# A graph network of 32 batch entries: eight groups of four become two, seven times four, and two

## The chip, the cores and the metric

The kernel runs on one core of one Trainium2 chip. The metric is the device time of one execution in microseconds (us). Before the change the median of 3 runs is 3128.19 us (3117.14 to 3134.04). A difference under 0.5% can't be told from no change.

A core has engines with instruction queues of their own, each worked off in order: PE (TensorE, matrix products; PEld is its weight load), DVE (VectorE), ACT (ScalarE), POOL (GpSimd) and SP (which only issues transfers). Transfers are issued from SP, ACT and POOL. POOL alone issues the indirect ones, which gather or scatter rows by a list of indices.

## What is computed

The input x has 32 batch entries of 512 nodes by 256 features; one adjacency matrix adj of 512 x 512 serves all of them, and about 1.6% of it is not zero besides its diagonal. Four layers follow one another:

```python
def gnn(h, A, W1, b1, W2, b2, Wa, ba, Wm, bm, beta1, beta2, beta3):   # layers 0 and 3
    pre_u, pre_v = h @ W1[:256], h @ W1[256:]
    hidden = relu(pre_u[:, :, None] + pre_v[:, None] + b1)             # per entry 512 x 512 x 256
    S = sigmoid(hidden @ W2 + b2)                                      # per entry 512 x 512
    a = einsum('buv,bud->bvd', S * A, h)
    m = einsum('uv,bud->bvd', A, h) * h
    return beta1 * h + beta2 * (a @ Wa + ba) + beta3 * (m @ Wm + bm)

x = gnn(x, adj, ...)                                                   # layer 0
x = x + relu((adj @ x) @ W.T + b)                                      # layer 1
f = x @ W1.T; g = f @ W2 + b2                                          # layer 2
x = softmax(leaky_relu(g[:, None] + g[None]) + adj) @ f + bias2 + x
x = gnn(x, adj, ...)                                                   # layer 3
```

S is needed only where adj is not zero, since it is multiplied by adj. The kernel computes it there alone, edge by edge.

## The kernel before

The 32 entries go in eight groups of four (`NB` = 4). A group passes through these stages; each is a Python generator, and each of its `yield`s ends a piece of instructions:

- `first` loads four entries of x, turns them on PE and calls `pre`, which computes pre_u and pre_v and writes them to a table in DRAM (`table`, one row per node, the four entries side by side: 4 KB a row). 16 table writes a group, from SP.
- `edges` (layer 0: `edges0`) computes S on the edges. The edges are held as 36 *items* of 128 edges (`ITEMS`): 32 from lists of each node's neighbours, and 4 from *panels*, which hold what overflows. The 36 don't depend on the size of the group: an edge list serves all entries, and a larger group only makes the rows longer. For each item POOL issues a gather (`fetch`, L607), DVE adds the two ends (L686), applies relu and W2 (L694 for all four entries at once, with the sums on ACT, L672; or L702 entry by entry with the sum on DVE), a sigmoid follows for some items together, and POOL issues a scatter (`put`, L601) of 128 values per entry into `cells`. These are two dense arrays in DRAM, one for each half of the rows of S*adj. The scatters of one half follow one another, each waiting for the landing of the one before it. The panels need a gather more each, for the other end of their edges (`mine`, by `iu`).
- `load` (L727) brings the dense S*adj back in four transfers of 1 MB, issued from POOL behind the scatters. `middle` then does the rest of layer 0, layers 1 and 2, and layer 3's `pre`, entry by entry (`middle_one`).
- `edges` again for layer 3 (`edges3`), a second `load`, and `last`, which finishes layer 3. For the last group of all, `last_before` computes the products that don't need S (`hWa`, `mhT`) during `edges3`, and `last_behind` does the sums (`sums`) after the load. In the same way `middle_before` computes `hWa` and `mhT` of the first group's four entries while its `edges0` run.

Only places of edges are ever written to `cells`, and every group writes the same places, so the arrays are set to zero once: `zeros` issues 8 transfers of 512 KB for each layer from SP, those of layer 0 in the setup.

The lists of edges come from `Edges.build`. It ranks each row's neighbours and writes rank and value to `lists` in DRAM (L312), then takes the items of the four chunks of nodes in the order 0, 2, 1, 3 (L316 to L343; eight items each, one DVE and one ACT instruction over 128x512 an item). After all four come the panels (L345 to L380): which node each line of a panel belongs to, by eight small matmuls and some ten small DVE instructions, a gather of that node's row of `lists` for each of the four panels (L368), and two DVE instructions for each.

The order on every engine comes from `weave`. Each stream of pieces has times in units of one group's middle stage (`spread`, `edge_times`, `middle_shares`), and the pieces are issued in order of these times. Streams marked "fill" are put where the middle stage has room. `behind` further holds back some DVE and ACT instructions of the edges until those of the middle stage issued two pieces before. The Tile framework then assigns semaphores and buffers, and lets queues that are free run ahead. Before the change `middle` of group t spans t - 0.47 to t + 0.53 (the first 0 to 0.53).

Of the kernel before, what the change touches and what calls it, by code (L numbers as in the profile page):

```python
# [16 lines left out]
P = 128  # L17
# [202 lines left out]
class Edges:  # L220
# [28 lines left out]
    def build(self, counts, adjT, lists, psum, big, tmp):  # L249
# [66 lines left out]
        for c in (0, 2, 1, 3):  # L316
            at = slice(c, c + 1)
# [26 lines left out]

        js = slice(NC * OWN, ITEMS)  # L345
        pu = psum()[:, 0 : 2 * PANELS]
        ones_bf = bf2[:, 1024:1025]
        nc.vector.memset(ones_bf, 1.0)
        for k in range(2 * PANELS):
            h, q = divmod(k, PANELS)  # L350
            mm(nc, pu[:, k : k + 1], [(full[:, h * 2 + c, q * P : (q + 1) * P], ones_bf) for c in range(2)])
        u, node, slot, start, sp, v, there, t = (sheet(2 * PANELS) for _ in range(8))
        nc.vector.tensor_scalar(u, pu, float(HALF - 1), None, ALU.min)
        nc.vector.tensor_copy(node, u)
        nc.vector.tensor_scalar(node[:, PANELS:], u[:, PANELS:], float(HALF), None, ALU.add)
        inode = self.inode
        nc.vector.tensor_copy(inode, node)
        nc.vector.tensor_scalar(self.iu, node, 2.0, None, ALU.mult)
        nc.gpsimd.iota(slot, [[0, 2], [P, PANELS]], 0, 1, allow_small_or_imprecise_dtypes=True)
        nc.vector.tensor_scalar(start, u, float(N), None, ALU.mult)  # L360
        nc.vector.tensor_scalar(sp, slot, float(CELLS + NC // 2 * OWN * P), None, ALU.add)
        nc.vector.tensor_scalar(t, slot, 1.0, None, ALU.add)
        yield
        gots = []
        for k in range(2 * PANELS):
            gots.append(tmp.tile([P, 2 * N], F32, name=f"got{k}", tag=("h1", "hT1", "mhT0", "hWa0")[k]))
            index = bass.IndirectOffsetOnAxis(ap=inode[:, k : k + 1], axis=0)
            nc.gpsimd.indirect_dma_start(out=gots[k], out_offset=None, in_=lists, in_offset=index)  # L368
        yield
        for k in range(2 * PANELS):  # L370
            at = slice(k, k + 1)
            rank, adj = gots[k][:, 0:N], gots[k][:, N:]
            junk = bf2[:, 2048 + k % 2 * N :][:, 0:N]
            nc.vector.scalar_tensor_tensor(
                junk, rank, t[:, at], adj, ALU.is_equal, ALU.mult, accum_out=self.value_of(NC * OWN + k)
            )
            nc.vector.scalar_tensor_tensor(junk, rank, slot[:, at], ones, ALU.is_le, ALU.mult, accum_out=v[:, at])
            yield
        self.slots(js, v, there, t, start, sp, 0)
# [19 lines left out]
class Group:  # L399
# [3 lines left out]
    def __init__(self, sp, w, name):  # L403
        self.w = w
        self.table = sp.dram.tile([2 * N, GROUP], F32, name=f"table_{name}")
        self.cells = sp.cells[name[0]]
        self.s = sp.grp.tile([P, ITEMS, NB], F32, name=f"s{name[0]}")
        self.self_s = sp.grp.tile([P, NC, NB], F32, name=f"self_s{name[0]}")
# [6 lines left out]
class Sparse:  # L415
# [3 lines left out]
    def __init__(self, ctx, m, counts, xr, outr, B):  # L419
# [7 lines left out]
            k: [self.dram.tile([CELLS + SPARE, NB], F32, name=f"cells_{k}{q}") for q in range(2)] for k in "03"  # L427
        }
        self.lists = self.dram.tile([N, 2 * N], F32, name="lists")
# [80 lines left out]
    def setup(self):  # L510
# [13 lines left out]
        self.zeros(self.cells["0"])  # L524
# [5 lines left out]
    def zeros_behind(self):  # L530
        self.zeros(self.cells["3"])
        yield

    def zeros(self, cells):
        for c in cells:
# [503 lines left out]
def even(n):  # L1039
    return [1.0] * n  # L1040
# [322 lines left out]
```

## Time and profile before

One profiled execution took 3102.14 us, its span is 3100.4 us. It is 26.05 us under the median of the runs.

| | busy us | share of the span |
|---|---|---|
| PE | 2714.6 | 88% |
| DVE | 2302.8 | 74% |
| POOL | 1522.5 | 49% |
| ACT | 1337.8 | 43% |
| TensorE clock granted, mean | 0.941 | |
| moved by DMA | 679.40 MB | 219 GB/s |

PE's busy time counts a matmul until its modelled end, and these overlap, so a busy PE can still do more. POOL's busy time is mostly that of issuing gathers and scatters, about 1.2 us each.

The fourth and last transfer of each `load` divides the span into stages. By their places in the queue the loads of layer 0 (groups 0 to 7) lie at 262, 474, 816, 1165, 1519, 1872, 2230 and 2584 us, those of layer 3 at 681, 1028, 1380, 1728, 2088, 2448, 2787 and 3042 us. The first gather of all starts at 83.13 us and the last group's first gather of layer 3 at 2885.63 us.

### The profile page before, as it was taken

Reading aid. Unit: us, or ns where it says so; the run is one execution under the profiler, and the core shown is the slowest. Engines: PE = TensorE matmul, PEld = TensorE weight load, DVE = VectorE, ACT = ScalarE, POOL = GpSimd, SP = SyncE. Lnnn points to the kernel's source line nnn. Section 1 sums busy time; section 2 is a strip of 40 time slices with the busy share of each in tenths; the row PEclk is TensorE's granted clock in tenths of the full one; section 3 lists DMA queues with packets and bytes.
Section 4 is the critical chain, followed back from the end, with each engine's and each line's share of the span. In section 5 each row is a group of like instructions: output and inputs, shape, how many; then the busy total and the mean of one; then the engine's idle time right before and its main releaser. Section 6 shows DMA issues by size and latency. Waiting matters only on the chain.

```text
span 3100.4 us, 32465 instructions
## 1 busy us (share of the span) xinstructions
PE 2714.6 (88%) x8645; PEld 1642.5 (53%) x8646; DVE 2302.8 (74%) x6026; ACT 1337.8 (43%) x4101; POOL 1522.5 (49%) x1312
## 2 busy tenths in 40 slices
PE   6366888889998999989998999989999899889957
PEld 3133444446654565546664565545664566545636
DVE  6783886889589875989589885888679795772761
ACT  3453554445345433545354442545335343453440
POOL 1462453556346563556346562565436563450561
PEclk9688988999999999999999999999999999999978
DMA  8874556786677766786668766787568766551753
GB/s 285 282 236 152 180 174 225 237 268 213 223 224 263 235 210 219 247 282 213 227 213 258 238 197 213 242 267 237 188 216 268 251 221 208 178 174 58 234 195 115
DMA packets 302719, 679.40 MB, mean 219 GB/s; under 512 B 52672, under 2 KB 170944, under 8 KB 294336
## 3 DMA queue, kind: packets, MB, share of 16 engines
q0 software_dynamic: 120384, 406.01, 41.0%
q1 hardware_dynamic: 163184, 234.01, 22.5%
q10 hardware_dynamic: 18960, 37.24, 3.2%
q8 instruction: 70, 1.15, 0.2%
q14 instruction: 121, 0.99, 0.1%
HBM read 531.12 MB, written 146.01 MB: 218 GB/s over the span
## 4 chain that ended last, share of the span: by engine, by line
PE 51%; DVE 18%; DMA 17%; issue 6%; ACT 4%; POOL 3%; SPq 0%; POOLq 0%; ACTq 0%; DVEq 0%
PE pst L45 24%; PE pst L1001 7%; DVE rows L686 6%; DMA table<-puv 5%; DMA rows<-table,iv 5%; PE pst L570 3%; DVE rows L702 3%; PE pst L861 3%; PE pst L1010 3%; PE pst L572 3%; DMA cells<-s,cell 3%; DVE rows L694 3%; PE pst L883 2%; PE pst L840 2%; DMA SA<-cells 2%
## 5 line engine op out<-in xcount | busy, mean ns | idle before, releaser
L601 POOL DMA_INDIRECT cells<-s,cell x576 | 691.1, 1200 | 740.7 <-DMA cells<-s,cell 370.3
L607 POOL DMA_INDIRECT rows<-table,iv x554 | 663.3, 1197 | 672.7 <-DMA table<-puv 148.1
L686 DVE TENSOR_TENSOR rows<-rows,mine 128x1024 f32<-128x1024 f32 x554 | 670.8, 1219 | 164.7 <-DMA rows<-table,iv 148.8
L672 ACT ACTIVATE rows<-rows 128x256 f32<-128x256 f32 x1096 | 442.9, 407 | 516.7 <-DVE rows L694 511.1
L45 PE MATMUL pst<-adj,h 128*128 128x512 f32 x1024 | 451.3, 592 | 0.3 <-PE pst L941 0.3
L702 DVE SCALAR_TENSOR_TENSOR rows<-rows,L_gnn_W2bc 128x256 f32<-128x256 f32 x1120 | 415.9, 419 | 1.8
L45 PE MATMUL pst<-L_gnn_Wa,hT 128*128 128x256 f32 x1024 | 264.3, 410 | 118.6 <-DMA hT<-xT 64.6
L694 DVE SCALAR_TENSOR_TENSOR rows<-rows,L_gnn_W2bc 128x1024 f32<-128x1024 f32 x274 | 332.3, 1216 | 0.3
L45 PEld LDWEIGHTS pst<-adj,h 128*128 128x128 f32 x1024 | 192.8, 190 | 222.4 <-issue 218.4
L45 PEld LDWEIGHTS pst<-L_gnn_Wa,hT 128*128 128x128 f32 x1024 | 207.7, 208 | 165.8 <-issue 53.1
L45 PE MATMUL pst<-eT,feats 128*128 128x512 f32 x512 | 231.5, 606 | 12.4 <-ACT eT L953 12.4
L45 PE MATMUL pst<-adjT,zW 128*128 128x512 f32 x512 | 227.8, 597 | 6.2 <-ACT zW L865 6.2
L1001 PEld LDWEIGHTS pst<-hWa,SA 128*128 128x128 f32 x896 | 213.7, 328 | 7.7 <-issue 4.5
L1001 PE MATMUL pst<-hWa,SA 128*128 128x256 f32 x896 | 216.8, 398 | 0.0
L861 PE MATMUL pst<-WT,hT 128*128 128x256 f32 x512 | 150.3, 459 | 75.9 <-DVE hT L848 75.9
L672 ACT ACTIVATION_READ_ACCUMULATOR rows<-rows 128x1 f32 x1096 | 206.7, 189 | 0.0
L809 ACT COPY flat<-SA 128x512 f32<-128x512 f32 x128 | 137.6, 1128 | 155.0 <-PE pst L45 60.1
L840 PE MATMUL pst<-flat,hWa 128*128 128x512 f32 x448 | 196.8, 592 | 0.0
L861 PEld LDWEIGHTS pst<-WT,hT 128*128 128x128 f32 x512 | 118.0, 235 | 114.9 <-DVE hT L848 88.1
L575 ACT COPY puv<-pst 128x256 f32<-128x256 f32 x256 | 93.7, 370 | 183.8 <-DVE puv L574 168.1
L574 DVE TENSOR_TENSOR puv<-pst,bc_L_gnn_b 128x256 f32<-128x256 f32 x256 | 105.0, 416 | 90.3 <-DMA table<-puv 53.8
L45 PEld LDWEIGHTS pst<-eT,feats 128*128 128x128 f32 x512 | 97.5, 193 | 127.5 <-issue 109.8
(170 smaller groups left out, 3979.3 us busy)
## 6 DMA issues: line engine op xcount, KB each, us to landing
table<-puv SPq DMA_DIRECT2D x256, 256.0 KB, 5.5
SA<-cells POOLq DMA_DIRECT2D x64, 1024.0 KB, 7.0
h<-in_x_dram SPq DMA_DIRECT2D x64, 512.0 KB, 6.4
mine<-table SPq DMA_DIRECT2D x64, 512.0 KB, 5.3
hT<-xT SPq DMA_DIRECT2D x36, 512.0 KB, 5.1
h<-x2s SPq DMA_DIRECT2D x36, 512.0 KB, 4.1
xT<-hT ACTq DMA_DIRECT2D x32, 512.0 KB, 5.5
x2T<-yT SPq DMA_DIRECT2D x32, 512.0 KB, 5.3
```

The costliest lines, as they stand in the source:

```text
L45: nc.tensor.matmul(out, lhsT, rhs, start=(n == 0), stop=(n == len(pairs) - 1))
L574: nc.vector.tensor_tensor(puv[:, 0, :], pp[:, 0:D], w["b1bc"], ALU.add)
L601: self.nc.gpsimd.indirect_dma_start(out=g.cells[half], out_offset=bass.IndirectOffsetOnAxis(ap=at, axis=0), in_=s, in_offset=None)
L607: self.nc.gpsimd.indirect_dma_start(out=rows, out_offset=None, in_=g.table, in_offset=bass.IndirectOffsetOnAxis(ap=at, axis=0))
L672: self.behind(nc.scalar.activation(part, part, AF.Identity, accum_out=g.s[:, k, b : b + 1]))
L686: self.behind(nc.vector.tensor_tensor(rows, rows, other, ALU.add))
L694: nc.vector.scalar_tensor_tensor(by_entry, by_entry, 0.0, w2, ALU.max, ALU.mult)
L702: nc.vector.scalar_tensor_tensor(part, part, 0.0, w["W2bc"], ALU.max, ALU.mult, accum_out=at)
L809: self.nc.scalar.copy(flat[:, r, :], SA[r][:, :, b])
L840: nc.tensor.matmul(pz, hWa[:, r, cs], flat[:, r, :], start=(r == 0), stop=False)
L861: nc.tensor.matmul(pw[:, at], zT[:, d, cs], m.WT_1[:, d, :], start=(d + k == 0), stop=(d * k == 1))
L1001: nc.tensor.matmul(pz[:, k * D : (k + 1) * D], SA[r][:, cs, b], hWa[:, r, :], start=(r + k == 0), stop=False)
```

## The change

The groups are now of 2, 4, 4, 4, 4, 4, 4, 4 and 2 entries: nine of them, of which the first and the last are small. Everything that depended on `NB` takes the group's own size `nb`. A small group has arrays `cells` of its own size, since a row of `cells` holds one value per entry; there are eight of these arrays where there were four. In `load`, two chunks of a small group share one tile. `first`, `middle_before`, `last_before` and `last_behind` at the ends do two entries for four. The number of items stays 36 for each group and layer.

The zeros of layer 0's small arrays (8 transfers of 256 KB) are issued from POOL in the setup, those of its large arrays from SP, a little later in the list of pieces; layer 3's are issued from POOL, behind a memset of the tile of zeros on DVE, during the first two middle stages.

The panels' lists move up: their matmuls, small DVE instructions and four gathers come after the items of chunks 0 and 2, ahead of those of chunks 1 and 3. What depends on the gathers stays behind all four chunks. In POOL's queue one of the four gathers now stands ahead of the first gather of rows and three behind the fourth; before, all four stood behind the twelfth gather of rows and the sixth scatter. In the first group a third spare buffer holds gathered rows.

The times of the pieces are set anew: the first middle stage takes 0.42 of a unit, the last one 0.5, the others 1; `first` of group 2 runs beside the first middle stage; `last` of group 6 ("last - 2") is spread over 0.8 of a unit, that of group 7 over 0.23.

```diff
@@ Edges.build
         for c in (0, 2, 1, 3):
+            if c == 1:
+
+                pu = psum()[:, 0 : 2 * PANELS]
...
+                    mm(nc, pu[:, k : k + 1], [(full[:, h * 2 + c, q * P : (q + 1) * P], ones_bf) for c in range(2)])
+                u, node, slot, start, sp, vp, therep, tp = (sheet(2 * PANELS) for _ in range(8))
...
+                yield
+                gots = []
+                two = tmp.tile([P, 2, 2 * N], F32, name="got", tag="eT")
+                for k in range(2 * PANELS):
...
+                    nc.gpsimd.indirect_dma_start(out=gots[k], out_offset=None, in_=lists, in_offset=index)
+                yield
             at = slice(c, c + 1)
@@ Group
-        self.table = sp.dram.tile([2 * N, GROUP], F32, name=f"table_{name}")
-        self.cells = sp.cells[name[0]]
+        self.table = sp.dram.tile([2 * N, nb * D], F32, name=f"table_{name}")
+        self.cells = sp.cells[name[0], nb]
@@ Sparse
         self.cells = {
-            k: [self.dram.tile([CELLS + SPARE, NB], F32, name=f"cells_{k}{q}") for q in range(2)] for k in "03"
+            (k, nb): [self.dram.tile([CELLS + SPARE, nb], F32, name=f"cells_{k}_{nb}_{q}") for q in range(2)]
+            for k in "03"
+            for nb in dict.fromkeys(sizes)
         }
@@ setup, zeros
-        self.zeros(self.cells["0"])
+        self.zeros(self.nc.gpsimd, "0", self.sizes[0])
...
     def zeros_behind(self):
-        self.zeros(self.cells["3"])
+        for nb in self.sizes[1:]:
+            self.zeros(self.nc.sync, "0", nb)
         yield
+        for nb in self.sizes:
+            self.behind(self.nc.vector.memset(self.zero, 0.0))
+            self.zeros(self.nc.gpsimd, "3", nb)
+            yield
@@ load
+        per = min(NB // nb, NC)
         for c in range(NC):
-            t = self.act.tile([P, N, NB], F32, name=f"SA{layer}", bufs=NC)
+            if c % per == 0:
+                tile = self.act.tile([P, N * NB], F32, name=f"SA{layer}", bufs=NC)
+            t = tile[:, c % per * N * nb : (c % per + 1) * N * nb]
@@ sparse_path
+    ends = [NB // 2] if B >= 2 * NB and B % NB == 0 else []
+    sizes = ends + [NB] * ((B - len(ends) * NB) // NB) + (ends or [B % NB][: B % NB])
...
-        (sp.zeros_behind(), spread(even(2), 0.15, 0.2), ""),
+        (sp.zeros_behind(), [-0.02] + [0.15 + 0.3 * k for k in range(len(sp.sizes) + 1)], ""),
...
-        start, end = (max(0.0, k - 0.47) for k in (t, t + 1))
+        start, end = end, end + (1.0 if not small else 0.5 if t else 0.42)
...
-            first = spread(FIRST, start - 0.86, start - 0.6)
-            edges0 = edge_times(start - 0.552, start - 0.505, start - 0.06, start - 0.04)
-        edges3 = edge_times(end + 0.003, end + 0.05, end + 0.48, end + 0.54)
-        behind = end + 0.56, end + 1.13
+            first = (0.1, 0.38) if t == 2 else (start - 0.86, start - (0.72 if small else 0.6))
+            at = start - (0.44 if small else 0.552)
+            edges0 = edge_times(at, at + 0.047, start - 0.06, start - 0.04)
+        edges3 = edge_times(end + 0.003, end + 0.05, end + (0.33 if small else 0.48), end + 0.54)
+        behind = end + 0.56, end + (0.85 if small else 1.13)
+        if t == last - 2:
+            behind = end + 0.6, end + 1.4
         if t == last - 1:
-            edges3 = edge_times(end + 0.003, end + 0.05, end + 0.46, end + 0.5)
-            behind = end + 0.7, end + 1.06
+            edges3 = edge_times(end + 0.003, end + 0.05, end + 0.46, end + 0.49)
+            behind = end + 0.55, end + 0.78
         if t == last:
-            end -= 0.2
-            edges3 = edge_times(end + 0.003, end + 0.02, end + 0.45, end + 0.46, LEAD_AT_ENDS)
-            behind = end + 0.29, end + 0.45
+            edges3 = edge_times(end + 0.003, end + 0.02, end + 0.28, end + 0.29, LEAD_AT_ENDS)
...
-            (sp.edges(g0, ("yT", "mhT3") if t == 0 else ()), edges0, ""),
+            (sp.edges(g0, ("yT", "mhT0", "hWa0") if t == 0 else ()), edges0, ""),
```

## The prediction

> **What bounds the kernel now.** I read the page first: PE's row says that matmuls fill most of the span, and the forty slices say where they don't: the first four and the last four. By the rows of groups, the edges cost POOL 1.2 us for each gather and scatter, and DVE and ACT by the length of the rows.
>
> ```profile
> PE 2714.6 (88%) x8645; PEld 1642.5 (53%) x8646; DVE 2302.8 (74%) x6026; ACT 1337.8 (43%) x4101; POOL 1522.5 (49%) x1312
> PE   6366888889998999989998999989999899889957
> ...
> L601 POOL DMA_INDIRECT cells<-s,cell x576 | 691.1, 1200 | 740.7 <-DMA cells<-s,cell 370.3
> L607 POOL DMA_INDIRECT rows<-table,iv x554 | 663.3, 1197 | 672.7 <-DMA table<-puv 148.1
> L686 DVE TENSOR_TENSOR rows<-rows,mine 128x1024 f32<-128x1024 f32 x554 | 670.8, 1219 | 164.7 <-DMA rows<-table,iv 148.8
> ...
> L694 DVE SCALAR_TENSOR_TENSOR rows<-rows,L_gnn_W2bc 128x1024 f32<-128x1024 f32 x274 | 332.3, 1216 | 0.3
> ```
>
> Then the view of busy time by stretches, cut at the loads of S*adj (start:end, length, busy of PE, PEld, DVE, ACT, POOL with counts, PE's granted clock, DMA share, GB/s):
>
> ```profile
> 0.00:83.00 83.00, 55.32 (x167) 29.78 (x169) 56.15 (x206) 31.89 (x82) 14.74 (x28) 0.92 0.84 286
> 83.00:262.00 179.00, 83.07 (x231) 45.70 (x228) 119.88 (x233) 82.52 (x345) 103.91 (x87) 0.75 0.74 257
> 262.00:474.00 212.00, 170.48 (x491) 91.78 (x492) 150.67 (x402) 103.35 (x276) 85.97 (x76) 0.87 0.48 151
> 816.00:1028.00 212.00, 195.92 (x609) 110.05 (x607) 168.31 (x465) 96.89 (x283) 104.49 (x90) 0.98 0.77 249
> 1028.00:1165.00 137.00, 134.68 (x467) 90.75 (x468) 114.09 (x300) 58.77 (x181) 83.93 (x71) 0.98 0.65 215
> 2885.00:3042.00 157.00, 110.86 (x356) 76.82 (x354) 104.05 (x133) 69.15 (x312) 98.21 (x79) 0.86 0.64 214
> 3042.00:3100.00 58.00, 46.02 (x188) 42.33 (x188) 9.78 (x14) 0.00 (x0) 1.12 (x2) 0.91 0.30 100
> ```
>
> In the middle (fourth and fifth line) PE is busy 92% and 98%: PE is the bound, and a period is 353.6 us (loads at 816 and 2584, five periods). In the second line (first group's edges, 179 us) and the sixth (last group's) PE has little to do, and no engine is full: POOL is nearest if its issue gap of 0.30 us per gather or scatter is added (104 + 76 x 0.3 = 127 of 179 us; 98 + 23 = 121 of 157). The waits of the second line's stretch (us in total, times, longest) show what is left of it, and the timeline how SP spends the setup:
>
> ```profile
> POOL cells L601 <- DMA cells<-s,cell: 23.4, 10, 5.0
> POOL rows L607 <- ACT rows L672: 10.0, 5, 3.7
> POOL cells L601 <- DVE puv L574: 9.4, 1, 9.4
> ```
>
> ```profile
> 23.86 4.20 SPq L538 DMA_DIRECT2D cells<-zero  x4
> 31.60 5.18 SPq L538 DMA_DIRECT2D cells<-zero  x4
> 38.14 0.61 SPq L582 DMA_DIRECT2D table<-puv  x1
> 45.36 0.43 DVE L574 TENSOR_TENSOR puv<-pst,bc_L_gnn_b 128x256 f32<-128x256 f32 x1 [4.51 <-DMA table<-puv]
> ```
>
> **PE's work per entry.** The chain of waits in the dense stretch 1036 to 1150 us shows eight 512-wide matmuls in 6.87 us and eight 256-wide ones in 3.45 us (7.47 us for the sixteen of L1001). An entry is then: `first` 7.8 (pre 6.87, turning 0.9); hWa and mhT 10.3; the rest of the middle 40.9; the last sums 10.9; hWa and mhT of layer 3 again 10.3. That is 80.2 us, 321 us a group, 91% of the period. PE work put off from an end costs 1/0.91 of itself later.
>
> **The start, stage by stage.**
>
> *To the first gather (83 us before).* Two entries are turned and tabled for four. In DVE's order the first add now has ahead of it, from 28 us on, 21 list instructions of 0.83 (L325 and its read), 10 puv, 8 both and 8 sums of 0.42 to 0.5, four L311 of 0.75 and some 25 small ones of 0.12: 35 us, so 63 us without stalls. The zeros: SP's eight of 12.9 us become three 512 KB ones ahead of the tables, 5 us; eight on POOL at 0.58 each (L727's mean) fall into 52.8 us in which POOL waits for the table. The moved panel block (8 small matmuls, some ten small DVE instructions, an iota) costs DVE 1 to 2 us; the gather now ahead of POOL's first rows waits for `inode` and all four list writes (before: issued by 47 us), and the rows queue behind it. I take 60 us; 55 if SP no longer stalls DVE, 70 if that gather comes late.
>
> *First group's edges.* Per item DVE goes from 2.44 (two of 1.22) to 1.4 (128x512 takes 0.68 in L848 and 0.75 in L325), ACT from 2.4 (four of 0.407 + 0.189) to 1.2; POOL stays. So POOL sets it: 127 us, plus waits. Of the three waits above the scatter's remains and those on DVE and ACT halve: I take 13 us, 140 us in all, load at 200. Bounds: 76 x (0.94 + 0.30) = 94 us at the shortest gather of the trace, 0.94 (rows between 0.935 and 2.038), plus 25; and the 179 of before less the 9.4 and 10.0: 120 to 160.
>
> The Trainium skill, page "GPSIMD Engine Reference", Key points, says that GpSimd shares its SBUF interfaces with VectorE and contends with DVE instructions that have two SBUF inputs, which the add is. The spread 0.935 to 2.038 us of one gather fits; by that rule halved adds would also shorten POOL's issue and the stage would lie near its lower bound, 120 us.
>
> *First middle stage with the second group's edges (212 us before).* This one doesn't shrink with the group in front. The 36 items are of full size: DVE 36 x 2.67 (1.22 plus the mean of 1.22 and 4 x 0.42) = 96 us, `first` of group 2 now beside it 22 us (16 x 1.35), two middles of some 13 us, small ones 4: 148 us, against 150.67 in the third line. At its beginning DVE waits some 25 us for PE's first product (`DVE hT L848 <- PE pst L847`, 24.4 us there). After that DVE was busy 81%, as in the fifth line (83%). PE has only two middles (82) and `first` (31) to offer, so it idles. With less of the middle to wait for I take 90%: 25 + 165 = 190 us, load at 390. Bounds: 25 + 148 = 173, and 220 (a little over before). Eight POOL issues and 0.95 us of memset for layer 3's zeros lie in POOL's idle time.
>
> *Next two stages.* Small edges of layer 3, POOL-bound: 20 us for the table (as between 816 and 837), then 115 for 36 items; then a full set as in the fifth line, 139 us. PE's 256 us fit in 275: load of group 2 at 665. Bounds 260 and 295.
>
> Before, that load lies at 816, but with more done: two middles (102.4), two `first` (15.6) and 1.1 `last` (21.2 each, by the pieces' times) more, 141 us of work, 155 at 91%. The start so gives 816 - 155 - 665 = -4 us: **nothing**, with -84 and +53 us at all bounds together.
>
> **The middle** repeats itself. The nine groups cost DVE some 17 us more (72 items at 2 x 1.45 against 2.67) and POOL 152 gathers and scatters, 182 us, beside a PE that is full and a POOL at 49%: I put it at nothing; in the two end groups it is counted.
>
> **The end.** Before, 516 us lie between the load of the last middle (2584) and the end, with work of four middles and 8.9 `last` (394 us). After, two middles and 8 `last` (272): 122 us less, 134 at 91%, so the mark to beat is 382 us. The steps: full-size edges of group 7 beside two middles, 203 us before with DVE busy 143.56; now DVE has 26 us less of middles and `first`: 182. Some 8 us to the first gather (5 before). The last edges, POOL-bound as in the start: 125 us (94 + 11 to 150) against 157; beneath them PE has 105 us (four `last`, two hWa and mhT), which fit only if the clock (0.86 here, 0.81 and 0.74 within) rises. Load 8. Sums: 58 us before for four (9 wait, 46 of PE), now 30 for two. 182 + 8 + 125 + 8 + 30 = 353: **29 us gained**; bounds 5 and 55.
>
> **The sum** against the profiled execution's own time, 3102.14: -29 + 4 = 3077, or 0.992 of it. It lies 26 us under the median; the median times 0.992 is 3103. I round to 3104.
>
> "DMA: Bandwidth & Descriptors" of the skill, section Issuing engines are not separate DMA queues, speaks against the moved zeros: transfers from several engines run on the same 16 DMA engines, and another issuer saves only its issue time. Here that is 9.4 us of SP; by the rule the DMA share of 0.84 in the first line stays, and the move is worth at most these 9.4.
>
> **The rivals.**
> 1. *The first middle is too short a cover* (slower). The second group's full edges take 235 us or more, since DVE waits for middle pieces and PE then has nothing to fill with. Against: 212 before, with twice the middle. For: DVE's work is the same 148. Price: at 215 the gain is gone; at 235 us the kernel is 20 us slower, at 260 it is 45: 3128 + 20 to 45, about 3160.
> 2. *No change*: the two ends give what the start takes, at 205 to 225 us there: 3118 to 3138.
> 3. *POOL at its floor* (large gain): both small edge stages at 105 to 115 us, the first middle DVE-bound at 173: 25 + 17 + 15 more, about 3045.
>
> **How the numbers follow.** Forecast (16 to 60 us gained) 0.42, rival 3 0.15, rival 2 0.16, rival 1 0.27. A measurement tells about 0.5%, 16 us, from none: faster 0.57, same 0.16, slower 0.27. The range leaves out half of rival 3's cases and the worst third of rival 1: 3055 to 3158; the forecast's own is 3068 to 3112.
>
> **What would show it.** First gather at 55 to 70 us; first load near 200; the second near 390 with DVE busy over 80% behind its first 25 us and PE under 70%; edges of the last group 115 to 140 us with POOL busy over 70%; 30 us from the last load to the end. I am wrong if the second load comes after 415, if the middle periods leave 354 us (POOL's extra work hurting there), or if PE, not POOL, ends the last stage.

## The result, and the profile after

The changed kernel takes 3211.74 us (median of 4 runs, 3202.82 to 3216.82) against 3126.41 us for the kernel before in the same set of runs: a ratio of 1.0271, 95% interval 1.0234 to 1.0309. It is slower by 85 us. In a later set of runs the same two kernels stood at 1.0345 (1.0307 to 1.0384). The prediction was 3104 us with a range of 3055 to 3158, so it was wrong in sign and range.

One profiled execution took 3214.26 us with a span of 3212.6 us, against the 3077 that the sum in the prediction gives for such an execution. These are lines of its page: the busy row, the slices, and the groups of scatters, gathers and adds.

```profile
PE 2734.0 (85%) x8645; PEld 1643.4 (51%) x8646; DVE 2324.5 (72%) x6364; ACT 1304.6 (41%) x3965; POOL 1675.2 (52%) x1496
PE   5456767988889997999889997999889997999569
...
L614 POOL DMA_INDIRECT cells<-s,cell x648 | 748.3, 1155 | 793.5 <-DMA cells<-s,cell 385.6
L620 POOL DMA_INDIRECT rows<-table,iv x624 | 737.6, 1182 | 527.8 <-DMA table<-puv 128.9
L699 DVE TENSOR_TENSOR rows<-rows,mine 128x1024 f32<-128x1024 f32 (+1 forms) x624 | 690.5, 1114 | 297.8 <-DMA rows<-table,iv 267.4
```

PE's busy time is nearly the same (2734 against 2715 us) in a span that is 112 us longer. POOL has 184 more instructions, 152 of them gathers and scatters, and these cost nearly as much each as before (1.16 and 1.18 us on average; 1.20 both before), although two groups in nine have rows half as long. DVE waits 298 us at its adds, nearly all of it for gathered rows; it was 165.

Busy time by stretches, cut at the fourth transfer of each load (start:end, length, busy of PE, PEld, DVE, ACT, POOL with counts, PE's granted clock, DMA share, GB/s):

```profile
0.00:66.00 66.00, 36.22 (x120) 19.86 (x122) 40.77 (x152) 23.31 (x59) 19.73 (x37) 0.90 0.84 288
66.00:216.00 150.00, 67.66 (x167) 34.78 (x165) 85.51 (x251) 55.56 (x211) 91.95 (x88) 0.71 0.68 198
216.00:397.00 181.00, 126.93 (x360) 66.07 (x361) 137.80 (x392) 71.69 (x230) 90.43 (x83) 0.85 0.65 208
397.00:547.00 150.00, 104.28 (x299) 57.83 (x298) 80.90 (x248) 57.12 (x150) 92.68 (x93) 0.86 0.60 191
547.00:713.00 166.00, 157.97 (x501) 92.33 (x501) 133.85 (x353) 73.74 (x220) 90.09 (x76) 0.96 0.64 191
919.00:1057.00 138.00, 137.95 (x476) 92.01 (x475) 112.12 (x295) 58.81 (x182) 84.49 (x72) 0.98 0.64 208
1057.00:1283.00 226.00, 195.37 (x599) 110.08 (x598) 169.28 (x467) 96.49 (x283) 103.68 (x88) 0.95 0.76 236
2839.00:3034.00 195.00, 166.54 (x520) 100.56 (x518) 138.06 (x368) 72.18 (x227) 93.87 (x81) 0.92 0.65 196
3034.00:3156.00 122.00, 76.19 (x229) 53.64 (x230) 60.31 (x125) 37.98 (x163) 83.35 (x81) 0.76 0.52 150
3156.00:3213.00 57.00, 51.93 (x221) 44.51 (x219) 11.39 (x17) 1.17 (x2) 0.52 (x1) 0.99 0.26 90
```

Read by the loads of layer 0, the change does at the start what it seems to: S of group 1 is loaded at 396 us instead of 474, and that of group 7 at 2502.6 instead of 2584.5, still 82 us ahead. But then a ninth group follows. From the load of group 7 to the end it is 710 us (336 to the load of group 8, then 374); before it was 516. The 194 us more eat the 82 and 112 besides, which is the difference of the two spans.

### The profile page after: what moved, and what is told of

The parts are those of the page before. It is cut to its first block, busy times and chain, and to the rows that moved or that the text cites. A ratio compares the mean times of both kernels' runs of the same rounds, so it can differ in the third digit from the quotient of the medians.

```text
span 3212.6 us, 32976 instructions
## 1 busy us (share of the span) xinstructions
PE 2734.0 (85%) x8645; PEld 1643.4 (51%) x8646; DVE 2324.5 (72%) x6364; ACT 1304.6 (41%) x3965; POOL 1675.2 (52%) x1496
## 4 chain that ended last, share of the span: by engine, by line
PE 42%; DMA 16%; DVE 14%; issue 5%; ACT 3%; POOL 3%; POOLq 0%; ACTq 0%; DVEq 0%
PE pst L45 19%; PE pst L1020 6%; DMA rows<-table,iv 5%; DMA cells<-s,cell 5%; DVE rows L699 4%; DVE rows L715 3%; DMA table<-puv 3%; PE pst L879 3%; PE pst L583 3%; PE pst L1029 2%; PE pst L585 2%; PE pst L901 2%; DVE rows L707 2%; DMA SA<-cells 2%; PE pst L858 1%
## 5 line engine op out<-in xcount | busy, mean ns | idle before, releaser
L614 POOL DMA_INDIRECT cells<-s,cell x648 | 748.3, 1155 | 793.5 <-DMA cells<-s,cell 385.6
L620 POOL DMA_INDIRECT rows<-table,iv x624 | 737.6, 1182 | 527.8 <-DMA table<-puv 128.9
L699 DVE TENSOR_TENSOR rows<-rows,mine 128x1024 f32<-128x1024 f32 (+1 forms) x624 | 690.5, 1114 | 297.8 <-DMA rows<-table,iv 267.4
L685 ACT ACTIVATE rows<-rows 128x256 f32<-128x256 f32 x1056 | 427.3, 407 | 615.7 <-DVE rows L707 597.6
L715 DVE SCALAR_TENSOR_TENSOR rows<-rows,L_gnn_W2bc 128x256 f32<-128x256 f32 x1200 | 445.8, 417 | 1.8
L707 DVE SCALAR_TENSOR_TENSOR rows<-rows,L_gnn_W2bc 128x1024 f32<-128x1024 f32 (+1 forms) x304 | 325.8, 1073 | 0.4
L1020 PE MATMUL pst<-hWa,SA 128*128 128x256 f32 x960 | 233.1, 400 | 11.3 <-ACT hWa L756 11.3
L858 PE MATMUL pst<-flat,hWa 128*128 128x512 f32 x480 | 210.9, 592 | 0.0
L970 PE MATMUL pst<-ident,ex 128*128 128x128 f32 x512 | 86.9, 302 | 100.8 <-DVE ex L931 91.7
L583 PE MATMUL pst<-w_L_gnn_W,hT 128*128 128x512 f32 x256 | 136.2, 657 | 29.2 <-ACT hT L570 26.9
```

The costliest lines, as they stand in the source:

```text
L583: nc.tensor.matmul(pp, hT[:, 0, ks], w["W1"][:, 0::DC, :], start=True, stop=False)
L614: self.nc.gpsimd.indirect_dma_start(out=g.cells[half], out_offset=bass.IndirectOffsetOnAxis(ap=at, axis=0), in_=s, in_offset=None)
L620: self.nc.gpsimd.indirect_dma_start(out=rows, out_offset=None, in_=g.table, in_offset=bass.IndirectOffsetOnAxis(ap=at, axis=0))
L685: self.behind(nc.scalar.activation(part, part, AF.Identity, accum_out=g.s[:, k, b : b + 1]))
L699: self.behind(nc.vector.tensor_tensor(rows, rows, other, ALU.add))
L707: nc.vector.scalar_tensor_tensor(by_entry, by_entry, 0.0, w2, ALU.max, ALU.mult)
```

## The experiments

Every ratio is against the kernel before in the same set of runs. "A period" is the mean from the load of layer 0 of group 3 to that of group 7 (four periods): 354.6 us before, 361.5 in the changed kernel.

### Is PE's work what a period costs? (e4)

```diff
-                for d in range(DC):
+                for d in range(DC if mhT is not None else 0):
...
-            for mhT in self.mhT(h, hT, 3):
+            for _ in range(DC):
                 yield
...
-            yield from self.sums(g, b, h, h, SA, hWa, mhT)
+            yield from self.sums(g, b, h, h, SA, hWa, None)
```

> The kernel before without the products adj@h and its product with Wm in layer 3 of the first seven groups (that part of the result is left out): 8 matmuls of 512 and 8 of 256 columns an entry, 6.87 + 3.45 = 10.3 us of PE, 41.3 us a group. If PE bounds the middle, as the prediction says, a period of 353.6 us falls by 41 to 45 us to 308 to 313, and the time by 270 to 310 us. If the chain of the two edge stages (POOL, DVE and the landings) bounds it, the period stays at 345 us or more and the time falls by less than 80 us. Between the two both share it: the period then says what PE work taken out, or put off into it, is worth.

Ratio 0.9876 (0.9829 to 0.9922): 38 us instead of 270 to 310. A period is 348.4 us. The busy row of its page, and a whole period by stretches:

```profile
PE 2505.8 (82%) x7749; PEld 1502.1 (49%) x7750; DVE 2258.9 (74%) x5970; ACT 1333.6 (43%) x4101; POOL 1542.3 (50%) x1312
```

```profile
1177.00:1381.00 204.00, 177.25 (x539) 99.20 (x538) 168.57 (x472) 93.88 (x281) 106.36 (x91) 0.96 0.80 253
1381.00:1529.00 148.00, 125.80 (x410) 82.95 (x408) 106.79 (x284) 60.98 (x183) 85.80 (x72) 0.90 0.65 210
```

PE's row counts 896 instructions less (448 matmuls, each of which the trace shows as two), and PE is busy 87% and 85% where it was 92% and 98%; the stretches are about as long as ever. So a full-looking PE wasn't what set the period: with a good tenth less to do it took nearly the same time. PE's busy time fell by 209 us, not by the 289 (28 entries of 10.3), as the mean clock granted fell from 0.941 to 0.911: 2714.6 - 289, times 0.941 / 0.911, is 2505.5 us, and 2505.8 were measured. The Trainium skill, page "TensorE: Matmul & The Clock Gate", section Part 1, says that the clock is gated by how busy the array has lately been; this agrees.

### What does a ninth group cost by itself? (e5, e15)

```diff
-    sizes = ends + [NB] * ((B - len(ends) * NB) // NB) + (ends or [B % NB][: B % NB])
+    sizes = [4, 4, 4, 2, 2, 4, 4, 4, 4]        # e5; the times at both ends as before
+    sizes = [4] * 7 + [2, 2]                   # e15; the start as before, the end as changed
```

The pieces of the small groups' middle stages are spread over 0.9 of a unit in e5; in e15 over 0.9 for the first of them and 0.5 for the last.

> Nine groups as in the changed kernel, but of 4, 4, 4, 2, 2, 4, 4, 4 and 4 entries: both ends are as before, and a group in the middle is split in two. No work of PE is added. If PE's work is what a period costs (the prediction), the time stays within 20 us of the sum of the parts alone, some 3100 to 3130 us. If the two sets of edges cost what they cost whatever PE does (theory A), three periods with one full and one small set, 142 + 100 to 130 us of gathers with 12 and 55 us between them, 310 to 340 us each, stand for two of 354: 220 to 310 us more, 3320 to 3420 us in all.

Ratio 1.0652 (1.0606 to 1.0699), 3323 us: 219 us above the parts alone (0.995, below), though no work of PE is added. The low end of theory A's range is nearly met, the other theory is 200 us off. The three periods concerned, 312, 306 and 309 us, take the place of two of 354. These are the first two:

```profile
1180.00:1388.00 208.00, 146.69 (x425) 83.67 (x424) 149.22 (x419) 71.99 (x242) 115.48 (x103) 0.85 0.69 219
1388.00:1492.00 104.00, 85.42 (x275) 55.92 (x273) 51.50 (x157) 25.73 (x78) 61.33 (x60) 0.90 0.48 142
1492.00:1668.00 176.00, 144.64 (x448) 86.08 (x448) 112.16 (x339) 58.97 (x183) 94.22 (x92) 0.90 0.66 196
1668.00:1798.00 130.00, 94.04 (x292) 58.14 (x292) 96.72 (x258) 42.01 (x143) 84.81 (x73) 0.85 0.64 210
```

No engine is full in any of them: PE 70 to 82%, DVE 50 to 74%, POOL 54 to 65% (69 to 82% with the gap of 0.30 us behind each of its instructions). The gathers of a full set of 36 items run over 135 to 146 us here, those of three of the four small sets over 118 to 122 (the first small set, beside a middle stage of four entries, took 139). Half the row length takes some 15% off a set.

Whether another order of the pieces would make a small group cheaper was not tried. By an estimate from these traces POOL alone needs some 103 us for the 76 gathers and scatters of a small set (1.06 us each and the gap of 0.30), so within a set of 118 to 122 us at most 15 to 19 us are in reach; what lies between the sets isn't bounded in this way.

> Nine groups: seven of four entries and then two of two. The start is as in the kernel before. Theory A from the runs so far: a small group inside costs some 287 us (574 for the pair in the middle), one at an end 234 (468 for the two of the changed kernel), a full one 354; so one inside and one at the end cost 521 for 354, 167 us more than the parts alone: 3240 to 3290 us, ratio 1.04 to 1.055. If PE's work were the cost, 3080 to 3130 us. The periods up to the load of group 6 are those of the question above: 358 to 361 us if the number of groups does it, 353 to 356 if the shift by two entries does.

Ratio 1.0314 (1.0265 to 1.0363), 3214 us. That is 114 us above the parts alone, below the range I had reckoned (167 us above, 3240 to 3290), and far from what PE's work alone would give. The changed kernel stands 101 us above the parts alone in its first set of runs and 124 in the later one. So a pair of small groups in place of one full group costs some 220 us more in the middle and 100 to 125 where one or both lie at the ends. To break even, a small group would have to cost 177 us, half of a period; in the changed kernel it costs 354 + 101 to 124, divided by two, 228 to 239.

### The smaller parts alone (e1)

Panels' lists sooner, zeros from POOL and the third spare buffer, with eight groups of four:

```diff
-        self.zeros(self.cells["0"])
+        self.zeros(self.nc.gpsimd, self.cells["0"])
...
-            (sp.edges(g0, ("yT", "mhT3") if t == 0 else ()), edges0, ""),
+            (sp.edges(g0, ("yT", "mhT0", "hWa0") if t == 0 else ()), edges0, ""),
```

> Eight groups of four as before, with the smaller parts of the change alone: lists of panels sooner, zeros from POOL, the third spare buffer in the first group. Theory A (the slowdown comes from nine groups and the short ends): 3105 to 3130 us here, first gather at 70 to 78 us instead of 83, five periods of 353 to 355 us in the middle. Theory B (the order in DRAM decides; here the tables of the groups lie as in the kernel before) expects the same. Theory C (the change of order in SBUF, which comes with the earlier gather of lists, slows the steady stages): periods of 358 to 362 us, the edge stages of layer 3 at 220 to 226 us, 3140 to 3180 us in all.

Ratio 0.995 (0.9931 to 0.9968): 15 us faster, and with e14 below, which has the same instructions and the same ratio, the fastest version here that computes all. A period is 353.8 us, so the changed order in SBUF (theory C) is not a cause. The start:

```profile
0.00:79.00 79.00, 52.82 (x176) 28.42 (x178) 52.68 (x197) 31.68 (x82) 19.89 (x37) 0.96 0.85 283
79.00:248.00 169.00, 85.93 (x220) 47.06 (x218) 122.21 (x242) 82.93 (x345) 108.69 (x88) 0.74 0.75 255
```

The first gather comes 4 us sooner than before and the first load 15 us sooner (248 against 263).

### Which engine does set the period? (e6, e7, e10, e13, e11)

> The kernel before, with every second scatter of S left out (so half of S is missing in the result). POOL has 18 x (1.2 + 0.3) = 27 us less to issue in a set, and the chain of scatters that wait for one another is half as long. If POOL and this chain set the pace of a set of edges, a set of 142 us takes 115 to 125, a period 300 to 330, and the time falls by 200 to 400 us. If DVE sets it, the periods stay within 5 us of 354 and the time within 50 us.

```diff
-                self.put(g, *r)
+                skip[0] = not skip[0]
+                if skip[0]:
+                    self.put(g, *r)
```

Ratio 0.9597 (0.9556 to 0.9638): 125 us, short of the 200 to 400. A period is 340.8 us. POOL's busy time fell by 323 us.

```profile
1126.00:1332.00 206.00, 196.94 (x617) 111.14 (x616) 167.64 (x465) 96.09 (x278) 84.34 (x71) 0.98 0.78 255
1332.00:1467.00 135.00, 130.56 (x463) 87.50 (x462) 113.19 (x300) 59.98 (x188) 65.70 (x56) 1.00 0.65 219
```

> The kernel before, with the sums of three items in four on ACT instead of every second one: in a set of 36 items of the middle, eight more go from DVE (4 x 0.42 = 1.68 us each, 1.22 instead) to ACT (2.4 us each). If DVE's work sets the pace of a set of edges, each set gets 3.7 us shorter, 14 sets 50 us: 3060 to 3080 us. If POOL and the landings of gathers and scatters set it, nothing: within 15 us of the kernel before; slower if rows now wait for ACT.

```diff
-            if spare or k % 2 == 1 and k < ITEMS - 3:
+            if spare or k % 4 and k < ITEMS - 3:
```

Ratio 1.0105 (1.006 to 1.0151): slower, with less work on DVE. That speaks against DVE, but ACT got more, so DVE's work had to be taken away outright:

> The kernel before, without the add of the two ends in every second item of the middle sets (16 of 36, 1.22 us each; their S is wrong): DVE has 19.5 us less to do in a set, 39 us in a period, about what the run without PE work took from PE (41 us, which gave 4.6 us a period) and the run with half of the scatters from POOL (54 us, 11 us a period). If DVE's own work sets the pace of the sets, a period falls by 25 to 39 us, the time by 170 to 280 us. If no engine's work does, but the order in which the queues wait for one another, it falls by 4 to 12 us a period, under 80 us in all.

```diff
-            self.behind(nc.vector.tensor_tensor(rows, rows, other, ALU.add))
+            if spare or k % 2 == 0 or k > ITEMS - 5:
+                self.behind(nc.vector.tensor_tensor(rows, rows, other, ALU.add))
```

Ratio 1.0928 (1.0887 to 1.0969): 290 us slower with 227 us less for DVE to do. Neither theory had this. The order of DVE's queue had changed: `behind` holds the add back behind pieces of the middle stage, and with the add gone nothing held back the multiplication after it (L694 of the kernel before, now L695), which the planner then placed ahead of pieces of the middle. There it waits for the gather, and what follows in the queue waits with it. First its row of the page of e10, then one place of DVE's timeline, where a piece of the middle (`mhT`) stands behind it:

```profile
L695 DVE SCALAR_TENSOR_TENSOR rows<-rows,L_gnn_W2bc 128x1024 f32<-128x1024 f32 x274 | 334.0, 1222 | 625.6 <-DMA rows<-table,iv 619.1
```

```profile
1307.25 1.22 DVE L695 SCALAR_TENSOR_TENSOR rows<-rows,L_gnn_W2bc 128x1024 f32<-128x1024 f32 x1 [9.06 <-DMA rows<-table,iv]
1308.39 0.68 DVE L751 TENSOR_TENSOR mhT<-pst,hT 128x512 f32<-128x512 f32 x1
```

e13 takes the same adds away and holds the multiplication back in their place:

> The kernel before, again without the add of the two ends in every second item of the middle sets (their S is wrong), but the multiplication that follows is now held back as the add was, so that DVE's order stays as before: 39 us less of DVE's work in a period. If DVE's own work is what a period costs, a period falls by 25 to 39 us and the time by 170 to 280 us. If the order in which the queues wait for one another is, as for PE (41 us taken, 4.6 gained) and POOL (54 taken, 11 gained), a period falls by 4 to 12 us and the time by 30 to 80 us.

```diff
-            self.behind(nc.vector.tensor_tensor(rows, rows, other, ALU.add))
+            added = spare or k % 2 == 0 or k > ITEMS - 5
+            if added:
+                self.behind(nc.vector.tensor_tensor(rows, rows, other, ALU.add))
...
-                nc.vector.scalar_tensor_tensor(by_entry, by_entry, 0.0, w2, ALU.max, ALU.mult)
+                made = nc.vector.scalar_tensor_tensor(by_entry, by_entry, 0.0, w2, ALU.max, ALU.mult)
+                if not added:
+                    self.behind(made)
```

```profile
L696 DVE SCALAR_TENSOR_TENSOR rows<-rows,L_gnn_W2bc 128x1024 f32<-128x1024 f32 x274 | 333.6, 1220 | 67.7 <-DMA rows<-table,iv 67.0
```

Ratio 0.9897 (0.9851 to 0.9943): 32 us faster, a period of 352.9 us. The wait of 626 us at the same instruction is 68 us.

| taken away | busy us less | whole time less, us | us gained for one of work |
|---|---|---|---|
| PE: products of layer 3 (e4) | 209 | 38 | 0.18 |
| POOL: half of the scatters (e7) | 323 | 125 | 0.39 |
| DVE: 16 of 36 adds a set (e13) | 226 | 32 | 0.14 |

The busy time is that of the pages against the profile of before, the gain that of the ratios. No one engine's work, taken away alone, comes back in full. POOL's comes nearest (that run also halves the chain in which one scatter waits for the landing of another). Since work was taken from one engine at a time, a second limit close behind the first isn't excluded: in e7 PE is busy 96% and 97% of the two stretches above, and what half of the scatters would give with room on PE is not shown. Six row buffers instead of five gave no gain either:

> The smaller parts of the change alone (eight groups of four), and six buffers for gathered rows instead of five, the gathers issued four items ahead instead of three (one buffer of the other ends' rows is given up for it). If the landing of gathers sets the pace of a set, a full set takes 128 to 137 us instead of 142 and the time falls by 60 to 120 us below the parts alone, to 0.96 to 0.975 of the kernel before. If it doesn't, the ratio stays near the parts' own 0.995, within 0.005.

```diff
-        self.act, self.small, self.gath = pool("act", 1), pool("small", 2), pool("gath", 5)
+        self.act, self.small, self.gath = pool("act", 1), pool("small", 2), pool("gath", 6)
...
-                t = self.gath.tile([P, GROUP], F32, name="mine", bufs=3)
+                t = self.gath.tile([P, GROUP], F32, name="mine", bufs=2)
...
-LEAD = 3
+LEAD = 4
```

Ratio 1.0109 (1.0076 to 1.0142): slower, with full sets of the middle of 153 to 162 us from the first gather to the last instead of some 142. The gathers of `rows` alone run over no more than before (134 to 145 us against 137 to 150); what comes late is the last of the four gathers of the other ends' rows (`mine`), which have two buffers here instead of three. In four periods (window 1028 to 2448 us) DVE's adds wait 68 us for `mine` and 43 for `rows`, in the kernel before 2 and 71. So the buffer given up hides what the sixth would do, and the question of the landings stays open.

### The end of the changed kernel (e8)

In the changed kernel PE idles in the last small set while work is left for after the last load. PE's timeline there (start, length, instructions, and in brackets the idle time before them and what ended it):

```profile
3052.15 6.51 PE L45 MATMUL pst<-L_gnn_Wa,hT 128*128 128x256 f32 x16 [25.85 <-DMA hT<-x2T]
...
3131.33 9.99 PE L1020 MATMUL pst<-hWa,SA 128*128 128x256 f32 x32 [11.35 <-ACT hWa L756]
...
3154.92 7.61 PE L1020 MATMUL pst<-hWa,SA 128*128 128x256 f32 x32
...
3187.04 7.07 PE L1020 MATMUL pst<-big,SA 128*128 128x256 f32 x32
```

The first line begins the second entry of the products in advance; from the third line to the last, where the sums of the last group begin, PE works off one and a half entries of group 7 in 32 us. (The expectation below says three, which was misread.) What the first line waits for, DVE's timeline shows:

```profile
3042.06 0.69 DVE L699 TENSOR_TENSOR rows<-rows,mine 128x512 f32<-128x512 f32 x1 [21.29 <-DMA rows<-table,iv]
...
3047.06 0.68 DVE L766 TENSOR_TENSOR big<-pst,hT 128x512 f32<-128x512 f32 x1
```

The first add of the last set stands in DVE's queue ahead of the multiplications that end the first entry's products, and waits 21 us for its rows. Only when the second of these has read hT, at 3047 us, can the next hT come into its buffer.

```diff
-            behind = end + 0.55, end + 0.78
+            behind = end + 0.5, end + 0.66
...
-            streams.append((sp.last_before(g3), spread(even(nb * AHEAD + 1), end + 0.005, end + 0.045), ""))
+            streams.append((sp.last_before(g3), spread(even(nb * AHEAD + 1), end + 0.2, end + 0.24), ""))
```

> The changed kernel, with the last stage of group 7 (four entries, 85 us of PE) put ahead of the two entries of products that the last group has done in advance, instead of behind them. In the changed kernel PE idles 46 of the 122 us before the last load, since the products in advance wait for the last group's x2T to come back from DRAM (33 us), and three entries of group 7 are left for after that load, which take 57 us to the end instead of the 38 I had predicted. If that is the cause, 15 to 20 us come back: 57 us become 37 to 42. If the edges set the end anyway, nothing changes (within 5 us).

```profile
3025.00:3151.00 126.00, 84.51 (x268) 61.04 (x268) 62.10 (x127) 36.87 (x161) 83.65 (x81) 0.78 0.49 146
3151.00:3209.40 58.40, 48.20 (x179) 35.70 (x177) 9.75 (x14) 2.35 (x4) 0.91 (x2) 0.92 0.28 96
```

Ratio 1.0303 (1.0241 to 1.0364), nothing gained: 58 us still follow the last load. PE idles 41 us ahead of it as against 46, and what stays behind is now the end of group 7's last entry and the products in advance. The wait for x2T that I had blamed is 5.6 us now, behind the load, and others stand in its place ahead of it: 7.3 us for `hWa` from ACT, as in the second line of PE's timeline above, 6.3 for the load of S, and 21.6 in 16 pieces for which the profile shows no cause. That ACT's and DVE's edges of the last set hold up PE's pieces is thus shown for a part of the idle time only. Another place for the adds was not tried.

### Five us a period more than before (e2, e3, e9, e12, e14, e16)

In the steady stages the changed kernel issues the same instructions in the same order as before, and yet a period is 361.5 us instead of 354.6.

> The kernel before, with four unused 1 MB arrays in DRAM (each gets one small write of zeros, 0.5 MB in all), so that the tables of the groups lie where the changed kernel has them, modulo 4 MB. Theory B (the place in DRAM slows the transfers of the steady stages): landings of the diagonal's write at 8.6 us instead of 6.0, edge stages of layer 3 at 220 to 226 us instead of 214, periods of 358 to 362 us, 3160 to 3190 us in all. Theories A and C: periods of 353 to 355 us, 3120 to 3140 us.

```diff
+        self.unused = [self.dram.tile([CELLS + SPARE, NB // 2], F32, name=f"unused{q}") for q in range(4)]
...
+        for t in self.unused:
+            self.nc.sync.dma_start(t[0:P, :], self.zero[:, 0 : NB // 2])
```

Ratio 1.001 (0.9991 to 1.0029), a period of 355.5 us: the place of the tables does nothing to the kernel before.

> The changed kernel, with its small arrays cells padded to 2 MB each, so that the tables lie as in the kernel before, modulo 4 MB. Theory B: steady periods back to 353 to 355 us from 358 to 361, 3160 to 3180 us in all against 3212. Theories A and C: periods of 358 to 361 us, 3205 to 3220 us.

```diff
-            (k, nb): [self.dram.tile([CELLS + SPARE, nb], F32, name=f"cells_{k}_{nb}_{q}") for q in range(2)]
+            (k, nb): [
+                self.dram.tile([max(CELLS * NB // nb, CELLS + SPARE), nb], F32, name=f"cells_{k}_{nb}_{q}")
+                for q in range(2)
+            ]
```

Ratio 1.0191 (1.0148 to 1.0235), a period of 358.5 us. The time is what theory B said, the periods aren't.

> The changed kernel with two more small transfers from SP in the setup (0.1 MB of zeros together, to lines that nobody loads). In the steady stages both kernels issue the same instructions in the same order, but a period is 358 to 361 us in the changed one and 354 before. One thing that differs is the count of transfers from SP and ACT that lie ahead, 6 more modulo 8, so that each transfer uses another one of the eight semaphores in turn. With the two more that count is as before. Theory D (this phase costs it): periods of 353 to 356 us, 20 to 40 us less than the changed kernel in the same set of runs. Otherwise periods of 358 to 362 us and the same time within 10 us.

```diff
         self.zeros(self.nc.gpsimd, "0", self.sizes[0])
+        for c in self.cells["0", self.sizes[0]]:
+            self.nc.sync.dma_start(c[CELLS : CELLS + P, :], self.zero[:, 0 : self.sizes[0]])
```

> The changed kernel itself, beside the others of this set on one chip: 1.023 to 1.031 of the kernel before, periods of 358 to 362 us from the load of group 3 to that of group 7.

1.0293 (1.0253 to 1.0334) with the two transfers and 1.0345 for the changed kernel beside it; periods of 358.9 and 360.0 us. Theory D falls.

> The changed kernel's code, with eight groups of four and the times of the kernel before, so the same instructions as in the run of the smaller parts alone, but with the tiles and arrays in the changed form. If the form of the code costs the 5 us a period: periods of 358 to 361 us, ratio 1.000 to 1.008. If the ninth group or the shifted entries do: periods of 353 to 356 us, ratio 0.990 to 0.998.

```diff
-    sizes = ends + [NB] * ((B - len(ends) * NB) // NB) + (ends or [B % NB][: B % NB])
+    sizes = [4] * 8                            # and the times of the kernel before
```

Ratio 0.995 (0.9923 to 0.9977), a period of 354.7 us: not the form of the code. In e15, with nine groups, the periods ahead of the small ones are 353.9 us: not the ninth group either. By elimination, what is left comes with the small group at the start.

> The changed kernel with another choice of entries: the small group at the start takes entries 0 and 1, the full groups take 4 to 7, 8 to 11 and so on as in the kernel before, and the small group at the end takes entries 2 and 3. The instructions are the same but for the addresses in DRAM. If the shift by two entries (1 MB in each of these arrays) costs the 5 us a period: periods of 353 to 356 us and 20 to 40 us less, a ratio of 1.016 to 1.026. If it is something else that comes with the small first group: periods of 358 to 361 us, ratio 1.027 to 1.035.

```diff
-        i += nb
+        i = 4 * t + 4 if t < last - 1 else 2
```

Ratio 1.0239 (1.0187 to 1.029), a period of 358.4 us: not the shift of the entries. The ratio itself lies in the range of the other theory and its interval reaches into both, but the versions of the changed kernel spread from 1.019 to 1.0345 while their periods all stay at 358 to 361.5, so I go by the periods. Some 4 to 7 us a period, 15 to 28 us over the four, come with the small first group by a way that stays open. The traces show where the time goes: over the four periods PE (1331 us against 1330) and DVE (1128 against 1127) are as busy in the changed kernel as before, but DVE waits 105 us for gathered rows instead of 73, and POOL 210 instead of 186 for the landing of scatters. Why these land later is not shown.

## Why the prediction was wrong

By its own steps:

- **What bounds the kernel: failed.** "PE is busy 92% and 98%: PE is the bound", says the prediction of the middle. e4 took 41 us of PE's work out of a period and the period lost 6. The stretch rows show how full PE is, and not what would happen with less.
- **The mark of equal work: the step that failed most.** The start was credited with "141 us of work, 155 at 91%" that the kernel before had done more by its load of group 2, and the end with 134: PE work put off was to cost 1/0.91 of itself, and a period with less of it to be shorter. By that mark the way from the load of group 2 to that of group 8 is 3077 - 1.7 - 353 - 665 = 2057 us. It was 2126, 69 us more. Six periods at before's 353.6 us, whatever PE has to do in them, are 2122. That this comes so near is in part luck: four of the six took 361.5 us on average, the two next to the small groups 344 and 336. An entry put off from an end isn't done in PE's spare time; it needs another turn of two sets of edges.
- **The middle "at nothing": failed with it.** The ninth group's 17 us more for DVE and 182 for POOL (without the gaps of 0.30 us, 46 more) were put at nothing since PE was taken to be full. A ninth group by itself costs 219 us in the middle (e5). No wait in the profile of before names this cost. The prediction's own sign of being wrong, middle periods that leave 354 us, came true (361.5), but makes up only some 28 us.
- **To the first gather, 60 us: nearly right.** 66.8 us, inside the bounds of 55 and 70.
- **First group's edges, 140 us: right but for size.** 148, inside 120 to 160; POOL is busy most (92 of 150 us, DVE 86). The load lies at 215 instead of 200. The skill's rule on shared SBUF interfaces ("GPSIMD Engine Reference", Key points) was to bring it near 120: it didn't, though its direction is seen. The median of a gather of `rows` in this stage is 0.97 us with rows of 2 KB and 0.99 with rows of 4 KB, but fewer take long: the mean of the stage's 81 gathers and scatters is 1.07 us against 1.22. In the trace of before, the 160 gathers and scatters beside which DVE is idle take 0.97 us on average, and the 591 beside which it works on two SBUF inputs for over 80% of their time 1.30. POOL's busy time is 12 us shorter here (92 against 104), but POOL still stood for 58 of the 150 us, in its gaps and in waits.
- **First middle stage, 190 us: right.** 181, and rival 1, which had this stage at 235 or more, is refuted in its place, though its 3160 us come nearest to the result.
- **Next two stages, 275 us: failed.** 150 and 166 where the terms were 135 and 139, outside 260 to 295 in sum. In the small set of layer 3 POOL takes up 121 of 150 us with its gaps, but it doesn't set the time alone: DVE, with short rows, overtakes the gathers and waits 40 us for them, with middle pieces behind it in its queue, and PE idles 46 us. The stage after it then has PE busy 158 of 166 us.
- **The end, 353 us: mis-sized.** 374: 195 for the edges of group 7 (182), 122 for the last ones (8 + 125), 57 after the last load (8 + 30). The last is the term that failed: one and a half entries of `last` (32 us) were still to do after the load. e15, which has nothing left there, ends 32 us after it, near the 38 that I had.
- **The smaller parts: right.** I had them worth a few us at the start; they are worth 15 in all (e1). Zeros from POOL left the DMA share ahead of the first gather at 0.84 (0.85 in e1, where they are as many as before), as the skill's section Issuing engines are not separate DMA queues ("DMA: Bandwidth & Descriptors") has it.

In sum 47 us at the start (15 and 41 late, 9 early), 69 in the middle and 21 at the end: 137, the whole gap from 3077 to 3214.

## What to carry to other kernels

A busy engine is not yet the bound: before work put off or taken away is given a price, take some away and look at the period, since here 0.14 to 0.39 us came back for each us of work on PE, POOL or DVE. Where every group goes through a fixed number of steps (here two sets of 36 items whatever its size), a smaller group at an end buys its shorter start with another turn of all the steps, which in the orders of pieces tried here cost more than it saved; count turns first, work second. And an experiment that removes an instruction can move the order of what is left, so look at the queue's order before its time is believed.

## What the runs showed that was not expected

- The order of DVE's queue alone is worth more than any engine's work: the same adds taken away give 1.093 in one order (e10) and 0.990 in the other (e13).
- Rows half as long leave the median gather on POOL as it was; only fewer of them take long. A set of edges gets some 15% shorter in the middle (118 to 122 us against 135 to 146), and more at the ends of the changed kernel: 111 us from the first gather to the last against 128 in e1 for the first set of all, 88 against 122 for the last.
- Taking matmuls away slowed the rest: 209 us of PE's busy time were freed where 289 were to go, and the granted clock fell from 0.941 to 0.911.
- The ratio of the same two kernels differed by 0.7% between two sets of runs (1.0271 and 1.0345, intervals that just touch), so differences of this size were judged within one set alone, or by the periods.
